# Bilinear block with channels on the partitions, and a mode sum with the products standing

## The chip, the cores and the metric

One core of one Trainium2 chip. The metric is the device time of one execution, in microseconds. TensorE is called PE below (PEld its weight loads), VectorE DVE, ScalarE ACT, GpSimd POOL, and SyncE, which only issues DMAs here, SP. All data is fp32; an fp32 matmul appears in the trace as two MATMUL records.

## The reference, cut to what matters

The input is 16 images of 56 x 56 pixels with 128 channels. Four residual blocks follow each other: windowed attention, a triangle product, a Fourier attention operator, and a bilinear block. Each is fed by a group norm. The two blocks that the change touches:

```python
# block 3 (Fourier): out is the attention-weighted sum over 32 heads, projd a spectral convolution of it
attn_w = softmax(q k^T)                                   # per head, 56 x 56
out    = einsum('bhts,bhsd->bhtd', attn_w, v)
projd  = irfft2(sum over heads of rfft2(out) * wP) + skip # the "mode sum", then the inverse transform
# ... two more spectral operators, each ending in an inverse transform

# block 4 (bilinear)
xp = silu(x @ W1) @ W2                                    # 128 + 16 + 16 channels: q (8 heads x 16), k, v
q, k, v = l2norm(q per head), l2norm(k), l2norm(v)
K_H1    = conv3x7(k, H1_w) + P1                           # per pixel 16 x 16
kernel  = einsum('xnk,xkd->xnd', q, K_H1)
feature = conv3x7(v, H2_w); V_G = conv3x7(v, G_w) + I     # per pixel 16 x 16 each
feature = einsum('xvw,xvd->xwd', V_G, feature)
out     = einsum('xnd,xvd->xvn', kernel, feature)         # 128 channels
```

## The kernel before, in words

`tile_blocks` loads constants and weights once, then runs the images one after the other: load and transpose, the four blocks, store. An image lies in SBUF as 128 channels by 3136 pixels; most loops run over 7 chunks of 448 pixels. SBUF and PSUM tiles come from rotating pools: `big` (6 tiles), `w8`, `w5`, `w4`, `w2`, `sm`, and in PSUM `psb` (4 single banks) and `psd` (2 pairs of banks). A framework places the waits and a scheduler fixes, at build time, the order of each engine's instructions; every engine then takes its queue in order. The order on PE is nearly that of the program, with a few later matmuls slipped in where an earlier one would wait.

`_fourier`. After the attention (L938 scores) the weights of 32 heads lie in `at` as 16 pairs. L979 makes the modes of the values (copied by ACT at L980, doubled to 112 partitions by one SBUF-to-SBUF DMA), L1005 and L1010 add the skip path. The mode sum: for each quarter q of 448 modes and each pair of heads, two DMAs spread the coefficient `table` over 56 partitions each, DVE or POOL (every third pair) makes three products of 448 (L1030, L1032: a complex product written with three real ones), and six matmuls (L1037) with the attention weights as the stationary operand (112 rows, 64 columns) sum them. Two pairs go to the two 64-column halves of PE. L1048 combines the three sums and L1051 folds the halves. `inverse` turns modes into pixels: L828 (32 stationary columns; neighbours in the order lie in different 32-column groups) and L839 (32 rows; neighbours in different row groups). It runs three times, the first time with one part in place of two.

`_bilinear`. First loop, the projections: per chunk L1107 (x W1, Silu on ACT), L1113 and L1114 (times W2, pixels on the partitions), squares and sums for the norms (L1117, L1118), the power -1/2 on POOL (L357, by way of `power`), scaling (L1127, L1128), transposes of k and v (L1131), a copy to `pad` (L1134), and 14 DMAs that build `im`, the 7-fold shifted image. Second loop, the products: per group of 112 pixels L1149 makes the three convolutions with pixels on the partitions, and `contract` runs three times, each a product of 2048 (L1160) and a reduction over 16 (L1161); the third product is POOL's. L1171 and L1172 add the residual.

Of the kernel before, what the change touches and what calls it, by code (L numbers as in the profile page):

```python
# [33 lines left out]
P = 128  # L36
# [49 lines left out]
def _constants():  # L86
# [71 lines left out]
    c["eyedup"] = ed  # L158
    c["fold"] = np.concatenate([np.eye(T), np.eye(T)], 0)
    c["unpair"] = ed.T  # L160
# [12 lines left out]
def _weights(i):  # L173
# [71 lines left out]
    wk3 = np.zeros((113, 3, 16, 16), np.float32)  # L245
    wv3 = np.zeros((113, 3, 2, 16, 16), np.float32)
    for u in range(16):
        for kw in range(7):
            wk3[u * 7 + kw, :, :, u] = h1[u, :, :, kw].T
            wv3[u * 7 + kw, :, 0, u, :] = h2[:, :, kw].T  # L250
            wv3[u * 7 + kw, :, 1, :, u] = gg[:, :, kw].T
    wk3[112, 1] = g["L3_conv_P1"][0].T
    wv3[112, 1, 1] = g["L3_conv_I"][0].T
    w["l3wk"] = wk3.reshape(113, -1)
    w["l3wv"] = wv3.reshape(113, -1)
# [17 lines left out]
def tile_blocks(ctx: ExitStack, tc: tile.TileContext, ins, out, at, stages=(0, 1, 2, 3)):  # L273
# [9 lines left out]
    w5p = ctx.enter_context(tc.tile_pool(name="w5", bufs=2))  # L283
    w8p = ctx.enter_context(tc.tile_pool(name="w8", bufs=3))
    w4p = ctx.enter_context(tc.tile_pool(name="w4", bufs=3))
    w2p = ctx.enter_context(tc.tile_pool(name="w2", bufs=6))
    smp = ctx.enter_context(tc.tile_pool(name="small", bufs=6))
# [14 lines left out]

    def w5():
        return w5p.tile([P, 3 * CH], F32, tag="w5", name=uid("w5_"))
# [50 lines left out]
    def power(dst, src, p, n):  # L355

        ptt(dst, src, C("mhalf")[:p, :n], ALU.pow)  # L357

# [300 lines left out]
def _fourier(env):  # L659
# [63 lines left out]
    table = e.dpool.tile([32, 4, 3, CH], F32, tag="table", name="table")  # L723
# [19 lines left out]

    stt(tmp, cvr, -1.0, cvi, ALU.mult, ALU.subtract)
    tt(cvi, cvi, cvr, ALU.subtract)
    for c, v in enumerate((cvr, cvi, tmp)):
        nc.sync.dma_start(out=table[:, :, c, :], in_=v.rearrange("p (c n) -> p c n", n=CH))
# [68 lines left out]
    def inverse(parts, consume):  # L816


        halves = [v.rearrange("p (l t) -> p t l", t=T) for v in parts]
        last = len(halves) - 1  # L820
        for k in range(2):
            ng = 4 - k
            p = e.psd()
            for i in range(8):
                for c, half in enumerate(halves):
                    for g in range(ng):
                        o = p[32 * g : 32 * g + 32, i // 4, i % 4 * TT : (i % 4 + 1) * TT]
                        mm(o, lhsT=half[:, 32 * k + 8 * g + i, :], rhs=C(f"di{c + 1}"), start=c == 0, stop=c == last)  # L828
# [4 lines left out]
            for g0 in range(0, ng, 2):  # L833
                gs = range(g0, min(g0 + 2, ng))
# [368 lines left out]
```

## Time and profile before

| | us |
|---|---|
| median of 3 runs | 23861.55 (23851.68 to 23864.71) |
| the profiled execution's own time | 23861.55 |
| its span, first to last instruction | 23859.8 |
| PE / DVE / POOL / ACT busy | 13641.5 / 12171.6 / 6721.9 / 3478.3 |
| mean granted clock of PE | 0.692 |

The profile page gives the busy time of each engine over the span, groups of instructions by line, and the idle time before each group with what ended it. Windows give the same busy times inside a stretch, with the clock that was granted to PE (1.00 is full speed, 0.50 half) and the DMA share. Busy time of PE counts overlapped matmuls once; the mean length of one is longer than the distance between two.

### The profile page before, as it was taken

The page shows a single profiled execution, that of the slowest core. Times are in us where ns is not written, and L with a number is a line of the kernel's source. Part 1 is how long each engine was busy: PE and PEld are TensorE (multiplying, and loading weights), DVE is VectorE, ACT ScalarE, POOL GpSimd, SP SyncE. Part 2 cuts the span into 40 slices and gives each one's busy share as a digit, 9 for nine tenths or more (in the row PEclk, how much of TensorE's full clock was granted, in tenths as well). Part 3 has the DMA queues.
Part 4 walks back from the last instruction along what each step waited for, and adds up shares of the span by engine and source line. Part 5 has one row for each costly group of instructions (what it writes and reads, how often), then busy time and mean ns, then how long its engine had stood idle before and what let it go on. Part 6 is the DMA issues. An engine that isn't in the chain of part 4 may idle for free. (4 is left out here: it accounts for less than half of the span.)

```text
span 23859.8 us, 190705 instructions
## 1 busy us (share of the span) xinstructions
PE 13641.5 (57%) x77186; PEld 7738.1 (32%) x77186; DVE 12171.6 (51%) x12638; ACT 3478.3 (15%) x6016; POOL 6721.9 (28%) x3295
## 2 busy tenths in 40 slices
PE   6556465564645647456475564745647456474564
PEld 4233242332423324233142332423324233242331
DVE  4364644646446464464644646446464464644646
ACT  2111121110211102111021110211102111021110
POOL 1322313133131331313313133131331313313133
PEclk7767676676766767667676676766767667676676
DMA  0202002020020200202011020110200102011020
GB/s 25 61 7 66 7 17 58 7 66 7 24 51 7 66 8 25 50 7 66 8 27 48 7 66 10 27 46 7 66 10 25 47 7 66 10 27 46 7 66 8
DMA packets 478015, 744.96 MB, mean 31 GB/s; under 512 B 259922, under 2 KB 361170, under 8 KB 475986
## 3 DMA queue, kind: packets, MB, share of 16 engines
q1 hardware_dynamic: 476994, 730.54, 12.3%
q8 instruction: 611, 10.01, 0.2%
q14 instruction: 266, 2.18, 0.0%
q10 hardware_dynamic: 144, 2.22, 0.0%
HBM read 648.35 MB, written 26.38 MB: 28 GB/s over the span
## 5 line engine op out<-in xcount | busy, mean ns | idle before, releaser
L1149 PE MATMUL psb<-wgt,big 113*112 113x256 f32 (+1 forms) x5376 | 2871.9, 704 | 2738.6 <-DVE w L1160 2281.6
L1161 DVE TENSOR_REDUCE w<-w 112x128 f32<-112x2048 f32 x1344 | 3031.6, 2282 | 1147.0 <-POOL w L1160 1101.5
L357 POOL TENSOR_TENSOR sm<-sm,cst 112x40 f32<-112x40 f32 (+2 forms) x272 | 1680.4, 6178 | 6467.2 <-DVE sm L374 2979.9
L1160 POOL TENSOR_TENSOR w<-w,w 112x2048 f32<-112x2048 f32 x448 | 2020.6, 4510 | 4324.3 <-DVE w L1161 4074.2
L1149 PEld LDWEIGHTS psb<-wgt,big 113*112 113x112 f32 x5376 | 1357.2, 265 | 4176.5 <-DVE w L1160 2605.2
L1037 PE MATMUL psd<-w,w 112*64 112x448 f32 x4096 | 1603.7, 661 | 343.8 <-POOL w L1032 322.1
L1030 DVE TENSOR_TENSOR w<-big,w 112x448 f32<-112x448 f32 x688 | 540.7, 788 | 1569.5 <-PE psd L1037 918.3
L1037 PE MATMUL psb<-w,w 112*64 112x448 f32 x2048 | 1083.2, 673 | 271.1 <-POOL w L1030 235.2
L1030 POOL TENSOR_TENSOR w<-big,w 112x448 f32<-112x448 f32 x336 | 399.2, 1188 | 2562.7 <-PE psd L1037 993.6
L1151 ACT COPY w<-psb 112x512 f32<-112x512 f32 x448 | 262.2, 585 | 5591.7 <-PE psb L1149 2950.1
L1160 DVE TENSOR_TENSOR w<-big,psb 112x2048 f32<-112x2048 f32 x448 | 1020.2, 2277 | 52.0 <-PE psb L1149 52.0
L1160 DVE TENSOR_TENSOR w<-w,w 112x2048 f32<-112x2048 f32 x448 | 1025.8, 2290 | 37.6 <-DVE w L1161 0.9
L536 PE MATMUL psb<-cst,w 128*49 128x128 f32 x2048 | 460.8, 418 | 849.8 <-DVE w L530 849.8
L1037 PEld LDWEIGHTS psd<-w,w 112*64 112x64 f32 x4096 | 418.1, 157 | 1432.3 <-POOL w L1032 593.3
L934 POOL TENSOR_TENSOR w<-w,coef 128x448 f32<-128x448 f32 x512 | 654.5, 1294 | 560.4 <-DVE head L935 296.7
L1032 DVE TENSOR_TENSOR w<-big,w 112x896 f32<-112x896 f32 x688 | 796.4, 1158 | 0.0
L938 PE MATMUL psd<-w,head 128*64 128x56 f32 x8192 | 642.9, 238 | 231.0 <-DVE head L935 231.0
L799 PE MATMUL psb<-cst,big 128*56 128x64 f32 (+1 forms) x5376 | 416.8, 254 | 620.0 <-ACT big L787 376.5
L654 POOL TENSOR_TENSOR big<-big,w 128x448 f32<-128x448 f32 x112 | 126.0, 1131 | 2166.7 <-DVE w L653 2166.7
L1032 POOL TENSOR_TENSOR w<-big,w 112x896 f32<-112x896 f32 x336 | 734.7, 2187 | 0.0
L1131 PE MATMUL psb<-cst,w 112*32 112x112 f32 x448 | 115.8, 382 | 1048.4 <-DVE w L1128 1048.4
L536 PEld LDWEIGHTS psb<-cst,w 128*49 128x49 f32 x2048 | 397.4, 201 | 905.9 <-issue 891.4
(241 smaller groups left out, 23018.2 us busy)
## 6 DMA issues: line engine op xcount, KB each, us to landing
w<-table SPq DMA_DIRECT2D x2048, 294.0 KB
big<-pad SPq DMA_DIRECT2D x1568, 28.0 KB
w<-x SPq DMA_DIRECT2D x112, 224.0 KB
out<-w SPq DMA_DIRECT2D x112, 224.0 KB
big<-big SPq DMA_DIRECT2D x16, 784.0 KB
cst<-cst SPq DMA_DIRECT2D x1, 2246.5 KB
wgt<-wgt ACTq DMA_DIRECT2D x1, 2170.5 KB
big<-late SPq DMA_DIRECT2D x4, 224.0 KB
```

The costliest lines, as they stand in the source:

```text
L357: ptt(dst, src, C("mhalf")[:p, :n], ALU.pow)
L536: nc.tensor.transpose(p[:WIN, i * P : (i + 1) * P], s3[:, 4 * g + i, :], C("ident"))
L799: mm(p[:T, i * 2 * nl : (i + 1) * 2 * nl], lhsT=src[:, t * T : (t + 1) * T], rhs=fc, start=True, stop=True)
L934: ptt(t3, xb, bc(coef[:, 1, h, :], 2, T), ALU.mult)
L938: mm(sp[half : half + 64, bank, col : col + T], lhsT=hd[:, l, :], rhs=yk[:, l, :], start=l == 0, stop=False)
L1030: eng.tensor_tensor(t[:TT, :CH], x3[0][:, s], tb[:TT, :CH], ALU.mult)
L1032: eng.tensor_tensor(t2, ri3[:, :, s], b2, ALU.mult)
L1037: mm(acc[k][64 * half : 64 * half + 64, :], lhsT=at[:, pair % 8, pair // 8, :], rhs=t[:TT, k * CH : (k + 1) * CH], start=two == 0, stop=tw ...
L1149: mm(p[:TT, :m], lhsT=t[:113, c0 : c0 + TT], rhs=W(w)[:, dr * m : (dr + 1) * m], start=dr == 0, stop=dr == 2)
L1151: nc.scalar.copy(fv[:TT, :], pv[:TT, :])
L1160: eng.tensor_tensor(t4, x, y, ALU.mult)
L1161: reduce(dst, t4, AX.X, ALU.add)
```

## The change

The words of the change speak of the bilinear block; the diff rewrites the mode sum and `inverse` too.

- Bilinear products: channels stay on the partitions. Each convolution (`conv`) gives 256 channels by 448 pixels as two matmul groups, copied by ACT. In `contract`, PE replicates each head-pair's 16 values over the partitions with a constant 0/1 matrix (`rep`, 32 rows), DVE multiplies straight from PSUM, and PE sums over 16 partitions with another (`red`, 32 columns). The three contractions are taken in a pipeline over the chunks. POOL has no product here any more.
- Projections: q comes with channels on the partitions; its norms are taken by a matmul with `heads` and applied at the very end. The power on POOL becomes `rsqrt`, ten small DVE operations.
- Mode sum: two real products in place of three, `table` with two parts; the product of 896 is the stationary operand (8 slices of 112 columns) and the attention weights move (56 columns). DVE makes the first part's product, POOL the second's. Two pairs of heads share a table DMA.
- `inverse`: the loop over the column groups is outside, so neighbours in the order lie in the same group; in the second step the two parts of one group follow each other.
- Pools: `w5` is gone, `w4` has 5 tiles, `sm` 8.

```diff
-    w5p = ctx.enter_context(tc.tile_pool(name="w5", bufs=2))
-    w4p = ctx.enter_context(tc.tile_pool(name="w4", bufs=3))
+    w4p = ctx.enter_context(tc.tile_pool(name="w4", bufs=5))
-    smp = ctx.enter_context(tc.tile_pool(name="small", bufs=6))
+    smp = ctx.enter_context(tc.tile_pool(name="small", bufs=8))
...
+    def rsqrt(dst, src, p, n):
...
+        ts(y.bitcast(I32), src.bitcast(I32), -0.5, float(0x5F3759DF), ALU.mult, ALU.add)
+        for i in range(3):
+            tt(t, y, y, ALU.mult)
+            stt(t, t, -0.5, src, ALU.mult, ALU.mult)
+            stt(dst if i == 2 else y, t, 1.5, y, ALU.add, ALU.mult)
...
     inverse:
-            for i in range(8):
-                for c, half in enumerate(halves):
-                    for g in range(ng):
-                        o = p[32 * g : 32 * g + 32, i // 4, i % 4 * TT : (i % 4 + 1) * TT]
-                        mm(o, lhsT=half[:, 32 * k + 8 * g + i, :], rhs=C(f"di{c + 1}"), start=c == 0, stop=c == last)
+            for g in range(ng):
+                for i in range(8):
+                    t = 32 * k + 8 * g + i
+                    o = p[32 * g : 32 * g + 32, i // 4, i % 4 * TT : (i % 4 + 1) * TT]
+                    for c in range(2):
+                        mm(o, lhsT=halves[c][:, t, :], rhs=C(f"di{c + 1}"), start=c == 0, stop=c == 1)
...
-            for g0 in range(0, ng, 2):
-                gs = range(g0, min(g0 + 2, ng))
-                ps = [e.psb() for _ in gs]
-                for c, name in enumerate(("fir", "fii")):
-                    for g, p in zip(gs, ps):
-                        s = slice(32 * g, 32 * g + 32)
-                        mm(p[:, :CH], lhsT=C(name)[s, :], rhs=v4[s, c], start=c == 0, stop=c == 1)
...
+            for g in range(ng):
+                s = slice(32 * g, 32 * g + 32)
+                p = e.psb()
+                mm(p[:, :CH], lhsT=C("fir")[s, :], rhs=v4[s, 0], start=True, stop=False)
+                mm(p[:, :CH], lhsT=C("fii")[s, :], rhs=v4[s, 1], start=False, stop=True)
...
     mode sum:
-                    eng = nc.gpsimd if n % 3 == 2 else nc.vector
...
-                    eng.tensor_tensor(t[:TT, :CH], x3[0][:, s], tb[:TT, :CH], ALU.mult)
...
-                    eng.tensor_tensor(t2, ri3[:, :, s], b2, ALU.mult)
...
-                            lhsT=at[:, pair % 8, pair // 8, :],
-                            rhs=t[:TT, k * CH : (k + 1) * CH],
...
+                for c, eng in ((0, nc.vector), (1, nc.gpsimd)):
+                    o = pair % 2 * 896 + c * CH
+                    t = e.w4()
+                    eng.tensor_tensor(
+                        t[:TT, :896].rearrange("p (l c r) -> p l c r", l=8, c=2),
+                        x4,
+                        bc(tb[:TT, o : o + CH].rearrange("p (l r) -> p l r", l=8), 2, 2),
+                        ALU.mult,
+                    )
+                    for l in range(8):
                         mm(
+                            acc[c][:TT, l * T : (l + 1) * T],
+                            lhsT=t[:TT, l * TT : (l + 1) * TT],
+                            rhs=at[:, pair % 8, pair // 8, :T],
...
     bilinear:
+    def conv(w, im, q):
+        t = e.w4()
+        for h in range(2):
+            p = e.psb()
+            for dr in range(3):
+                c0 = (8 * q + dr) * T
+                mm(p[:, :CH], lhsT=W(w)[:, (2 * dr + h) * P : (2 * dr + h + 1) * P], rhs=im[:113, c0 : c0 + CH], start=dr == 0, stop=dr == 2)
+            nc.scalar.copy(t[:, h * CH : (h + 1) * CH], p[:, :CH])
+        return t[:, : 2 * CH].rearrange("p (h t) -> p h t", h=2)
+
+    def contract(y, z):
+        acc = e.psb()
+        for n in range(2):
+            prods = []
+            for two in range(2):
+                p = e.psd()
+                for i in range(2):
+                    s = slice(64 * two + 32 * i, 64 * two + 32 * i + 32)
+                    mm(p[:, i, :CH], lhsT=C("rep")[s, n * P : (n + 1) * P], rhs=y[s], start=True, stop=True)
+                t = e.w8()
+                t4 = t[:, : 4 * CH].rearrange("p (i h t) -> p i h t", i=2, h=2)
+                tt(t4, bc(p[:, :, :CH], 2, 2), bc(z, 1, 2), ALU.mult)
+                prods += [t4[:, 0], t4[:, 1]]
+            for h in range(2):
+                for i, t in enumerate(prods):
+                    mm(
+                        acc[32 * i : 32 * i + 32, :CH],
+                        lhsT=C("red")[:, (2 * n + h) * 32 : (2 * n + h + 1) * 32],
+                        rhs=t[:, h],
...
-            for a in range(4):
-                n = 4 * q + a
-                pk, pv = e.psb(), e.psb()
-                for p, t, w, m in ((pk, im[0], "l3wk", 256), (pv, im[1], "l3wv", 512)):
...
-                contract(nc.vector, kern, bc(q4[:, n], 2, D), bc(k3, 1, NH))
-                contract(nc.vector, s3, bc(kern, 2, D), bc(f3, 1, NH))
-                contract(nc.gpsimd, o3, bc(s3, 1, D), bc(g3, 2, NH))
...
+        for q in range(NCH + 2):
+            if q < NCH:
+                kern[q] = evacuated(contract(qc[:, q * CH : (q + 1) * CH], conv("l3wk", im[0], q)))
+            if 0 <= q - 1 < NCH:
+                feat[q - 1] = evacuated(contract(kern.pop(q - 1), conv("l3wf", im[1], q - 1)))
+            if 0 <= q - 2:
+                last(q - 2, feat.pop(q - 2))
```

In the projections, two wide matmuls a chunk (W2 with 128 columns) give q with channels on the partitions, and twelve short ones give k, v (32 columns) and the sums of squares of q (8 columns). `evacuated` is an ACT copy out of PSUM; `last` adds four transposes and a DVE product with the norms of q.

## The prediction

> **What bounds the kernel now.** I read the page's busy line first, then the busy time in stretches of one image, then the costliest groups, the waits inside the two stages that change, and the timeline.
>
> ```profile
> span 23859.8 us, 190705 instructions
> PE 13641.5 (57%) x77186; PEld 7738.1 (32%) x77186; DVE 12171.6 (51%) x12638; ACT 3478.3 (15%) x6016; POOL 6721.9 (28%) x3295
> ```
>
> No engine is full: each stage has its own bound. Stretches of the second image (us; busy PE, PEld, DVE, ACT, POOL; granted clock; DMA share; GB/s), in order: work ahead of the mode sum, mode sum, first inverse transform, bilinear projections, bilinear products:
>
> ```profile
> 1987.50:2065.90 78.40, 70.56 (x309) 57.09 (x309) 13.65 (x20) 12.88 (x23) 4.40 (x4) 0.50 0.10 26
> 2065.90:2261.00 195.10, 149.41 (x441) 44.29 (x440) 81.34 (x91) 4.26 (x8) 68.94 (x42) 0.87 0.71 183
> 2261.00:2276.20 15.20, 10.32 (x140) 6.86 (x140) 5.46 (x9) 1.06 (x2) 0.00 (x0) 0.72 0.00 1
> 2504.80:2633.20 128.40, 61.64 (x166) 25.05 (x166) 17.14 (x49) 14.98 (x26) 47.19 (x7) 0.59 0.11 16
> 2633.20:3037.00 403.80, 190.33 (x399) 94.16 (x398) 324.47 (x164) 20.96 (x37) 127.80 (x33) 0.67 0.04 10
> ```
>
> The last stretch is VectorE's: 324 of 404 us busy, the rest mostly waits for POOL's product (63 us in that stage's waits). Its groups (the last one by shape, inside 2504.8 to 2633.2):
>
> ```profile
> L1161 DVE TENSOR_REDUCE w<-w 112x128 f32<-112x2048 f32 x1344 | 3031.6, 2282 | 1147.0 <-POOL w L1160 1101.5
> L1160 DVE TENSOR_TENSOR w<-big,psb 112x2048 f32<-112x2048 f32 x448 | 1020.2, 2277 | 52.0 <-PE psb L1149 52.0
> L357 POOL TENSOR_TENSOR sm<-sm,cst 112x40 f32<-112x40 f32 x7 | 47.2, 6741 | 80.2 <-DVE sm L1119 80.2
> ```
>
> The projections are one serial chain per chunk, 18.0 us from one L1107 to the next in the timeline, 6.74 of it POOL's power. The mode sum is spread over DMA (0.71), PE, VectorE and POOL.
>
> [...] The trace agrees on the two states, but shows which work counts as busy (start, length, then the columns above):
>
> ```profile
> 1990.00:2010.00 20.00, 20.00 (x109) 20.00 (x108) 1.14 (x1) 3.67 (x7) 0.00 (x0) 0.50 0.00 1
> 1935.00:1975.00 40.00, 29.62 (x402) 26.16 (x401) 40.00 (x46) 0.00 (x0) 27.94 (x23) 1.00 0.01 1
> ```
>
> The first is L979 (56 rows, 112 columns moved): PE is never idle, yet stays at half. The second, L938 (128 rows), has gaps and full clock. Columns moved[...], times rows used: [...] 0.22 of full-speed capacity; [...] 0.47. I tallied the granted-clock record in its 3.41 us steps, leaving out lines whose tiles run side by side: of 1378 half-clock steps below 0.30 none was followed by full clock; at 0.35 to 0.375, 8 in 10 were. Of full-clock steps at 0.40 or more, nine in ten stayed. [...] L1051, 112 stationary and 56 moving columns, gives the price of such a stream:
>
> ```profile
> 2210.82 1.75 PE L1051 MATMUL psb<-cst,w 128*112 128x56 f32 x16 [1.41 <-DVE w L1048]
> 8050.06 3.02 PE L1051 MATMUL psb<-cst,w 128*112 128x56 f32 x15 [1.41 <-DVE w L1048]
> ```
>
> An fp32 matmul is two records here. Start to start, 98 ns at full clock ((1.75 - 0.262)/15), 187 ns at half ((3.02 - 0.393)/14)[...]. [...] matmuls on different 32-column groups run together[...]. L828 agrees: 560 records an image in 23.1 us busy, 41 ns each at 317 ns long. [...]
>
> **The change, per image (16 of them, one after the other).**
> *Mode sum.* Out: 192 matmuls of 448 columns, POOL's third of the products, a third of the table's bytes. In: 4 x 16 pairs x 2 parts x 8 = 1024 matmuls, 2048 records of 112 stationary, 56 moving columns. VectorE's product of 896 costs 1.16 us a pair (L1032), POOL's 2.19: 140 us a stage; table DMA, two thirds of 195 x 0.71 = 139, is 92 us. PE is last whatever its clock: 2048 x 187 = 383 us at half, 2048 x 98 = 201 at full. Which? At half the stream counts [...] 0.22: never raised in the tally. At full it counts 0.42: kept. So the entry decides, and the stretch ahead is at 0.50; its matmuls (L979, L1005, L1010) stay, and the order lists put nothing else among the new ones. I take half: 384 with the evacuation, against 195.1, less some 3 us by which the stretch ahead gets shorter (a few of the sum's matmuls were issued inside it): +186. If at full: 202, so +4. Bounds: these two, as a stream that is kept or never raised has no third state. Products and DMA issues (SP's table loads fall from 128 to 64 an image) are hidden by this PE stream; POOL's 140 us would show only if PE took less. The three-way sum at the stage's end (L1048, L1051, L1052, 3 us a quarter) and POOL's 4 additions L987 go; they are inside the 195.
> *Inverse transforms (three).* Now all 16 matmuls of one column group precede the next group's, so they no longer overlap; the first also gets 112 in place of 56. 224 records x 98 = 22.0, plus some 45 records at half clock at the two starts (+4), plus the second step, whose row groups now follow each other: 5 + 4 slots of 0.75 = 6.8, copies between 1.7: 34.5 us each. Before, L828 to L839 measured 12.8, 13.9 and 13.5 (means of 16). +63. Bounds: +30 if groups still overlap in part, +85 at half clock throughout.
> *Projections.* PE's order takes the chunks strictly one after the other, transposes last, so the chain's length is the pitch and each wait holds the next chunk's L1107 behind it. POOL's 6.74 goes; in its place ten small VectorE operations in a row, 0.2 each (L1119 0.18) = 2.0. L1113/L1114 (3.9) become four wide records at clock mixed (2.2) and 24 short ones (2.5 to 4), with two ScalarE passes (0.8 exposed). With L1107 (3.4), the reduction and its neighbours (1.1), one broadcast product (0.3) and the transposes (1.3) the chain is 3.4 + 2.2 + 0.8 + 3.0 + 1.1 + 2.0 + 0.3 + 1.3 = 14.1 to 14.5 in place of 18.0: 7 x 3.7 = -26. The 98 im2col DMAs and their order on SP stay. Bounds -40 and -5.
> *Products.* Out: VectorE's 84 reductions and 56 products, POOL's 28. In: 21 contractions, each 4 VectorE products (8.1 us), 6 convolution, 8 replicating and 16 summing matmuls of 448 columns, 0.75 each at full clock alone: 6 x 0.75 = 4.5; 8 in pairs on different rows 3.0; 16, which the order splits into 2 and 6 at a time, 4.5: 12.0. Both engines hand work back and forth through two PSUM pairs. PE takes its queue in order, so a sum that waits for a product holds the replications and convolutions queued behind it, and VectorE waits for those. Following the listed order at full clock: products 1 and 2 end at 3.0 and 5.0, 3 at 7.1, 4 at 9.6 (its replication waits behind six sums), the last sums at 11.1, then five convolution matmuls, on which the next product waits: 14.8. Its count is (4.5 x 113/128 + 3.0 x 0.5 + 4.5)/14.8 = 0.67, so full clock mostly; some steps fall (the first 3.4 us count 0.32): 15.5. 21 x 15.5 = 326, transposes and final products 14, next image's load and start 12: 352, against 404 (first L1149 to the next image's L481): -52. Bounds: 12.3 a contraction if the queues overlap (-119); 24 at half clock (+126).
> The rest (constants, one-time table, deeper pools; the other stages' order is the same but for VectorE swaps): nothing; these run in chains, so a freed buffer is no one's last wait; at most 5 either way.
> Sum: 186 + 63 - 26 - 52 = +171; x 16 = 2736. On the profiled execution's 23861.55 us (span 23859.8 and 1.75 around it; it is the median run too): 26,600.
>
> **The rivals.** *A: full clock in the mode sum* (ends faster). For: at full the stream would hold itself. Against: the 0.50 at entry. With the first inverse also starting at full (-5): +4 + 58 - 26 - 52 = -16 an image: 23,600. It decides from a mean record spacing of 104 ns: then the stage is 213 us and the image even. *B: contractions overlap*, 12.3 us: 67 less an image, 25,500. For: two PSUM pairs; against: the order's blocks. *C: contractions at half clock*, PE 24 us each: 29,450. For: L1149 now sits at 0.67; against: dense 448-column work.
>
> **How the numbers follow.** Main 0.62 (own range 25,700 to 27,700), A 0.13, B 0.17, C 0.08. PREDICTED is main's time. The range 24,600 to 27,900 takes B and the bounds of inverses and projections and leaves out A, C and main's tails. No change means within 0.2%, 48 us, about what measurement can tell: only A's edge, 0.02. Faster 0.11, slower 0.87.
>
> **What would show it.** Clock 0.50 and one unbroken PE stream of about 384 us in the mode sum; inverses of some 34 us; projection chunks near 14; contractions of 15 to 16 with VectorE half idle. A mode sum near 200 us, or contractions away from 12 to 18, makes it wrong.

## The result, and the profile after

The changed kernel takes 27,052.9 us (median of 4 runs, 27,007.5 to 27,080.6) against 23,856.6 us (4 runs, 23,833.5 to 23,864.7): 1.134 times the time, 95% interval 1.132 to 1.1359. The prediction was 26,600 us, range 24,600 to 27,900. Direction, range and the main mechanism hold; two terms of the sum are off by more than 20 us an image, in opposite directions.

The page of the changed kernel: TensorE is busy for 20,702 us in place of 13,642, VectorE and POOL for less than before.

```profile
span 27005.7 us, 278225 instructions
PE 20702.2 (77%) x121154; PEld 14441.2 (53%) x121154; DVE 9763.5 (36%) x12268; ACT 3813.4 (14%) x6800; POOL 4892.4 (18%) x3023
```

The stretches of the second image that answer to those of before (us; busy PE, PEld, DVE, ACT, POOL; granted clock; DMA share; GB/s), in the same order: work ahead of the mode sum, mode sum, first inverse, projections, products:

```profile
2182.60:2258.20 75.60, 65.63 (x299) 56.17 (x298) 12.61 (x18) 12.88 (x23) 4.11 (x2) 0.50 0.09 22
2258.20:2640.80 382.60, 382.60 (x2050) 382.45 (x2050) 68.25 (x63) 3.73 (x7) 128.67 (x62) 0.50 0.24 60
2640.80:2675.00 34.20, 25.56 (x254) 22.72 (x254) 10.62 (x11) 1.59 (x3) 0.00 (x0) 0.85 0.00 0
2923.30:3030.60 107.30, 80.90 (x260) 44.20 (x261) 22.29 (x104) 18.95 (x40) 0.00 (x0) 0.61 0.12 19
3030.60:3434.00 403.40, 346.88 (x1343) 111.58 (x1342) 187.66 (x116) 37.92 (x72) 2.47 (x7) 0.84 0.04 10
```

Read the second line first: PE is busy for all of its 382.6 us, and the clock that was granted meanwhile is 0.50. The last line is the one that surprised: the same length as before, but now PE is busy for 347 of 403 us and VectorE for 188, and the clock is 0.84, not full. The costliest groups:

```profile
L1041 PE MATMUL psb<-w,w 112*112 112x56 f32 x32768 | 6120.6, 393 | 0.0
...
L1114 DVE TENSOR_TENSOR w<-psd,w 128x1792 f32<-128x1792 f32 x1344 | 2689.2, 2022 | 2770.6 <-PE psd L1111 2272.9
...
L1118 PE MATMUL psb<-w,cst 128*32 128x448 f32 x10752 | 2259.6, 687 | 751.8 <-DVE w L1114 746.7
```

The mode sum (L1041) alone is 6,121 us, with no idle time ahead of it. VectorE's products (L1114) have as much idle time ahead of them as work, and it is the replications L1111 that end most of it; the sums L1118 in turn wait for those products. Two engines wait for each other.

By stages, from the first and last matmul of each stage in the two traces, mean over the images, in us:

| stage of one image | before | after | change | predicted |
|---|---|---|---|---|
| window attention and triangle | 373.6 | 373.7 | +0.1 | 0 |
| scores to the end of the skip path | 144.9 | 145.0 | +0.1 | -3 |
| mode sum | 194.7 | 382.4 | +187.7 | +189 |
| three inverses | 40.2 | 80.0 | +39.8 | +63 |
| projections | 128.1 | 106.6 | -21.5 | -26 |
| products, store, next load | 404.1 | 395.3 | -8.8 | -52 |
| whole image | 1488.1 | 1685.7 | +197.6 | +171 |

(The +186 of the prediction is the second and third row together; the stages that are not listed change by 0.2 together.) 197.6 x 16 = 3,162, against 3,146 between the two profiled spans.

### The profile page after: what moved, and what is told of

Its sections match the earlier page's. It is cut to its first block, busy times and chain, and to the rows that moved or that the text cites. A ratio compares the mean times of both kernels' runs of the same rounds, so it can differ in the third digit from the quotient of the medians.

```text
span 27005.7 us, 278225 instructions
## 1 busy us (share of the span) xinstructions
PE 20702.2 (77%) x121154; PEld 14441.2 (53%) x121154; DVE 9763.5 (36%) x12268; ACT 3813.4 (14%) x6800; POOL 4892.4 (18%) x3023
## 5 line engine op out<-in xcount | busy, mean ns | idle before, releaser
L1041 PE MATMUL psb<-w,w 112*112 112x56 f32 x32768 | 6120.6, 393 | 0.0
L1041 PEld LDWEIGHTS psb<-w,w 112*112 112x112 f32 x32768 | 6117.8, 307 | 1.7
L1114 DVE TENSOR_TENSOR w<-psd,w 128x1792 f32<-128x1792 f32 x1344 | 2689.2, 2022 | 2770.6 <-PE psd L1111 2272.9
L1034 POOL TENSOR_TENSOR w<-big,w 112x896 f32<-112x896 f32 x1024 | 2136.7, 2087 | 5224.7 <-PE psb L1041 3602.6
L1118 PE MATMUL psb<-w,cst 128*32 128x448 f32 x10752 | 2259.6, 687 | 751.8 <-DVE w L1114 746.7
L363 POOL TENSOR_TENSOR sm<-sm,cst 128x56 f32<-128x56 f32 (+1 forms) x160 | 925.1, 5782 | 7328.6 <-DVE sm L393 4645.9
L1098 PE MATMUL psb<-big,wgt 113*128 113x448 f32 x4032 | 1725.0, 570 | 0.0
L1118 PEld LDWEIGHTS psb<-w,cst 128*32 128x32 f32 x10752 | 416.3, 123 | 2308.8 <-DVE w L1114 1253.7
L1098 PEld LDWEIGHTS psb<-big,wgt 113*128 113x128 f32 x4032 | 753.6, 198 | 930.9 <-issue 916.9
L843 PEld LDWEIGHTS psd<-cst,big 112*32 112x32 f32 x10752 | 1002.1, 139 | 101.8 <-DVE big L865 56.3
L843 PE MATMUL psd<-cst,big 112*32 112x112 f32 x10752 | 1035.7, 270 | 22.9 <-DVE big L865 22.9
L1111 PE MATMUL psd<-w,cst 32*128 32x448 f32 x3584 | 847.1, 641 | 0.0
L950 PEld LDWEIGHTS psd<-w,head 128*64 128x64 f32 x8192 | 655.5, 168 | 227.0 <-DVE head L947 197.6
```

The source lines that it names most:

```text
L843: mm(o, lhsT=halves[c][:, t, :], rhs=C(f"di{c + 1}"), start=c == 0, stop=c == 1)
L950: mm(sp[half : half + 64, bank, col : col + T], lhsT=hd[:, l, :], rhs=yk[:, l, :], start=l == 0, stop=False)
L1034: eng.tensor_tensor(t[:TT, :896].rearrange("p (l c r) -> p l c r", l=8, c=2), x4, bc(tb[:TT, o : o + CH].rearrange("p (l r) -> p l r", l=8 ...
L1041: mm(acc[c][:TT, l * T : (l + 1) * T], lhsT=t[:TT, l * TT : (l + 1) * TT], rhs=at[:, pair % 8, pair // 8, :T], start=pair == 0 and l == 0, ...
L1098: mm(p[:, :CH], lhsT=W(w)[:, (2 * dr + h) * P : (2 * dr + h + 1) * P], rhs=im[:113, c0 : c0 + CH], start=dr == 0, stop=dr == 2)
L1111: mm(p[:, i, :CH], lhsT=C("rep")[s, n * P : (n + 1) * P], rhs=y[s], start=True, stop=True)
```

## The experiments

Theory: (1) the mode sum is slow only because it is entered at half clock and its stream (112 rows, 56 columns moved for each 112 loaded) can't raise it; (2) the inverses lost overlap by the order of their matmuls; (3) the contractions lose by TensorE's waits for products, and more than the waits themselves, since the clock falls in them. Rivals stand in each expectation. All runs start from the changed kernel unless they say otherwise; the kernel before took 23,846.5 to 23,867.2 us beside them. The stage means of the runs, in us an image, read from their traces as above:

| run | mode sum | inverses | projections | products | image |
|---|---|---|---|---|---|
| changed kernel | 382.4 | 80.0 | 106.6 | 395.3 | 1685.7 |
| burst, 128 rows | 209.4 | 78.3 | 106.8 | 398.2 | 1515.1 |
| burst, 56 rows | 392.4 | 80.1 | 106.9 | 396.8 | 1697.1 |
| bilinear block alone | 195.7 | 38.8 | 106.7 | 395.5 | 1461.7 |
| inverse as before | 382.4 | 39.2 | 106.7 | 396.1 | 1643.3 |
| convolution early | 382.4 | 79.7 | 107.2 | 332.8 | 1624.0 |
| deeper order | 382.4 | 80.0 | 106.8 | 287.9 | 1578.2 |
| filler of four | 382.4 | 80.3 | 105.9 | 408.7 | 1700.0 |
| filler of two | 382.4 | 79.8 | 107.1 | 387.1 | 1677.9 |
| all three edits | 209.3 | 36.7 | 105.7 | 287.7 | 1358.2 |
| before's Fourier, deeper order | 195.9 | 38.9 | 105.9 | 289.0 | 1351.6 |

(A burst is counted in the mode sum. The kernel before has 194.7, 40.2, 128.1, 404.1 and 1488.1.)

### The entry clock of the mode sum

```diff
         p12 = e.big()
+        p = e.psb()
+        for i in range(6):
+            mm(p[:, :CH], lhsT=C("cen"), rhs=xa[:, i * CH : (i + 1) * CH], start=True, stop=True)
         for q in range(4):
```

> Added to the changed kernel: six 128-row, 448-column matmuls right ahead of the mode sum of each image, into a PSUM tile that nothing reads. Theory (the mode sum stays at half clock only because it is entered at half, and its 56-row stream can hold full clock but not regain it): granted clock in the mode sum 0.9 to 1.0, spacing of its records 98 to 105 ns in place of 187, the stage 205 to 215 us in place of 382, the burst itself 5 to 10 us, so about -165 us an image: 24,400 us, between 24,200 and 24,700. Rival 1 (this stream cannot hold full clock whatever it is entered at): the clock falls back to half within some 10 us, the stage stays at 375 to 385 us, and the burst comes on top: 27,050 to 27,250. Rival 2 (the spacing is set by something other than the clock, the products or the table's transfers): clock full, but spacing above 130 ns: 25,500 or more.

(The stream that this expectation calls 56-row has 112 rows and moves 56 columns.) Measured: 24,191.6 us (24,149.6 to 24,276.2, 4 runs; 1.0141 of before, 1.012 to 1.0162), 8 us under the theory's band. The windows of its second image, ahead of the burst, the burst, the mode sum (columns as above):

```profile
2010.00:2085.50 75.50, 65.45 (x298) 55.89 (x297) 12.64 (x19) 12.74 (x23) 4.10 (x2) 0.50 0.09 22
2086.05:2093.50 7.45, 7.42 (x13) 3.61 (x14) 0.00 (x0) 0.00 (x0) 0.00 (x0) 0.62 0.00 0
2093.50:2295.00 201.50, 201.50 (x2050) 201.44 (x2049) 85.56 (x62) 3.72 (x7) 129.07 (x62) 1.00 0.45 113
```

The control uses 56 rows of the same matmuls (`C("cen")[:T]`, `xa[:T, ...]`).

> The control of the burst: the same six matmuls of 448 columns at the same place, but over 56 rows in place of 128; nothing reads their result. Theory (the clock is granted by moved columns weighted by their rows, and 56 of 128 rows at half clock are a share of 0.22): the clock stays at 0.5, the mode sum at 382 us, the burst adds some 9 us an image: 27,150 to 27,250 us. Rival (any stretch in which TensorE is busy without a gap gives full clock): as with 128 rows, 24,200 to 24,700. Second rival (it was only a shift in time that helped): both bursts the same.

Measured: 27,177.8 us (2 runs; 1.1388 of before, 1.1365 to 1.1411), 125 us over the changed kernel. Its second image, the same three stretches:

```profile
2200.00:2275.50 75.50, 65.54 (x298) 56.04 (x298) 12.60 (x18) 12.89 (x23) 4.12 (x2) 0.50 0.09 22
2276.20:2285.50 9.30, 9.29 (x13) 3.88 (x13) 0.00 (x0) 0.00 (x0) 0.00 (x0) 0.50 0.00 0
2285.50:2668.00 382.50, 382.50 (x2050) 382.40 (x2050) 67.70 (x62) 3.72 (x7) 128.92 (x62) 0.50 0.23 60
```

In both runs PE is busy without a gap in burst and mode sum, and the 2048 records of the mode sum are the same. The only difference is how many rows the six matmuls used. With 128 the clock is 1.00 for all of the next 201.5 us (98 ns a record), with 56 it is 0.50 for all of 382.5 (187 ns). Theory 1 holds: the entry decides, the stream keeps the clock that it finds, and being without gaps did not raise the clock (0.50 over all of the 382.5 us); the rows of the burst did.

Two further runs give the dose. In one the burst has another length in each image, in the other six matmuls use another number of rows in each image:

```diff
+        p = e.psb()
+        for i in range((0, 1, 2, 3, 4, 5, 6, 8)[b % 8]):
+            mm(p[:, :CH], lhsT=C("cen"), rhs=xa[:, i % 7 * CH : (i % 7 + 1) * CH], start=True, stop=True)
```

```diff
+        p, n = e.psb(), (56, 64, 72, 80, 88, 96, 104, 112)[b % 8]
+        for i in range(6):
+            mm(p[:, :CH], lhsT=C("cen")[:n], rhs=xa[:n, i * CH : (i + 1) * CH], start=True, stop=True)
```

> The changed kernel with a burst ahead of the mode sum (128 rows, 448 columns, read by nobody) of another length in each image: 0, 1, 2, 3, 4, 5, 6 and 8 matmuls in images 1 to 8, and again in images 9 to 16. At half clock one takes 1.5 us, and the granted clock is recorded in steps of 3.41 us. Theory (one step in which the moved columns, weighted by rows, are over about 0.35 of the full rate turns the clock up; a burst step gives up to 0.5, the mode sum's own 0.22): no image with 0 or 1 turns (382 us), those with 3 or more all turn (200 to 212 us), with 2 it depends on how the burst falls on the steps; 10 to 12 of 16 images turn, total 27,053 - 175 x 10 to 12: 24,950 to 25,350 us. Rival (the burst must last over two steps or more, some 7 us): only 5, 6 and 8 turn, 6 of 16 images, 26,000 us.

> The changed kernel with a burst of six 448-column matmuls ahead of the mode sum (read by nobody) over another number of rows in each image: 56, 64, 72, 80, 88, 96, 104 and 112 in images 1 to 8, and again in images 9 to 16. Theory (the share is 0.5 x rows / 128 at half clock, and about 0.35 is needed): 56 to 80 rows (0.22 to 0.31) do not turn the clock, 96 to 112 (0.375 to 0.44) do, 88 (0.34) either way; 6 to 8 images of 16 turn, total 27,178 - 183 x 6 to 8: 25,700 to 26,080 us. Rival 1 (it takes all 128 rows): none turns, 27,180. Rival 2 (anything over the stream's own 56 rows is enough, for it is the change that counts): 14 turn, 24,620.

Measured, one run each: 25,239.7 and 26,062.7 us, both in the theory's bands. The mode sums, read from the trace image by image, fall on two values with nothing between:

| burst | images | mode sum, us |
|---|---|---|
| 0, 1 or 2 matmuls of 128 rows | 6 | 382.4 to 382.5 |
| 3 matmuls | 2 | 202.0, 202.1 |
| 4, 5, 6 or 8 matmuls | 8 | 201.5 |
| six of 56, 64, 72, 80 or 88 rows | 10 | 382.4 to 382.5 |
| six of 96, 104 or 112 rows | 6 | 201.5 |

As the windows of the run with lengths show it (image 3, two matmuls; image 4, three):

```profile
3958.90:4341.30 382.40, 382.40 (x2050) 382.26 (x2048) 67.74 (x62) 3.72 (x7) 128.54 (x62) 0.50 0.24 60
5643.10:5845.20 202.10, 202.10 (x2050) 202.03 (x2049) 85.66 (x62) 3.72 (x7) 129.03 (x62) 1.00 0.44 113
```

and of the run with rows (image 5, 88 rows; image 6, 96):

```profile
7364.80:7747.20 382.40, 382.40 (x2050) 382.30 (x2049) 67.72 (x62) 3.72 (x7) 128.71 (x62) 0.50 0.24 60
9063.00:9264.50 201.50, 201.50 (x2050) 201.44 (x2049) 87.70 (x62) 3.72 (x7) 131.67 (x62) 1.00 0.45 113
```

At half clock 88 rows are a share of 0.5 x 88/128 = 0.344 and 96 rows 0.375, so the turn lies between these two, at or a little above the 0.35 of the tally of before. The clock is recorded in steps of 3.41 us, and full clock began on a step's boundary, 3.6 or 5.6 to 5.9 us after the burst's first matmul. Three matmuls take 4.6 us and turned the clock in both images that had three. Two take 3.1 us, nearly as long as a step, but in both images a boundary cut them in two: the steps that hold the parts have shares of 0.32 and 0.30 in the one image, 0.33 and 0.29 in the other. Two that lie within one step would give it (0.5 x 2.98 + 0.22 x 0.43)/3.41 = 0.46, an estimate from these figures (one takes 1.49 us at half clock); no run has that case.

The traces allow a sharper tally than the prediction's. Take each step of 3.41 us and give it this share: the time in which columns move, times the rows in use out of 128, times the granted clock, over the step. A column of a record takes 0.84 ns at full clock and 1.67 ns at half: in the changed kernel, records of 448 columns on 113 rows (L1098) start 376 and 747 ns apart (medians). (Matmuls that run side by side count their rows once if they share them, as on different column groups, and added up if they do not; starts are moved by 0.1 us.) In these traces the next step is then at full clock when the share is 0.375 or more and at half when it is less, whatever the clock was before, with 271 exceptions in 102,980 steps. All 14 traces together:

| clock of a step | its share | steps | next step at full clock |
|---|---|---|---|
| half | under 0.375 | 49,085 | 156 |
| half | 0.375 or more | 10,136 | 10,108 |
| full | under 0.375 | 10,237 | 23 |
| full | 0.375 or more | 33,522 | 33,458 |

The 0.375 and the shift were fitted on the traces of the two kernels (41 exceptions in 14,867 steps); the other 12 follow them (230 in 88,113). All but 23 of the exceptions lie within 0.015 of 0.375. So in these traces one line serves for rising and falling, and the one step ahead is enough to tell. The mode sum lies below the line at half clock (0.5 x 56 x 1.67/187 x 112/128 = 0.22) and above it at full (56 x 0.84/98 x 112/128 = 0.42), and it kept either: 0.50 for 382.5 us, 1.00 for 201.5. The prediction's shares for L979 and L938 follow from the same times: 0.5 x 56/128 = 0.22, as 112 columns at 1.67 ns fill the 187 ns from one record to the next, and 402 x 56 x 0.84 ns in 40 us = 0.47.

### One half of the change alone

> The bilinear block of the change with the Fourier block of before, so one half of the change alone; two image pads in the bilinear block in place of three, and the pools of before (three 4 KB tiles in place of five), because the two blocks do not fit side by side otherwise. Theory (the two halves of the change are independent, as the stage table of the two traces says: projections -21.4 us, products -8.8 us an image): 23,857 - 16 x 30 = 23,370 us, between 23,200 and 23,500. Rival 1 (my prediction's own sizes, -26 and -52 us, hold when the Fourier block of before leaves clock and buffers as they were): 22,600. Rival 2 (the third pad and the fourth and fifth 4 KB tile carried the gain): within 0.3% of before, 23,800 to 23,900.

The edit puts `_fourier`, its table and its `w5` pool back, and fits the pools (`w4` 3, `sm` 6, `pads` 2). Measured: 23,421.0 us (4 runs; 0.9813 of before, 0.9796 to 0.9829), 51 over the theory's figure (the window attention and triangle, 377.6 us an image in place of 373.6, are more than that). Projections 106.7 and products 395.5 us are those of the full change, so the halves are independent: the bilinear block gains some 440 us, the Fourier block loses some 3,600. Rival 1, the prediction's own sizes, is out by 800 us. The gain is there without the deeper pools (rival 2).

### The order in the inverses

```diff
-            for g in range(ng):
-                for i in range(8):
...
-                    for c in range(2):
+            for i in range(8):
+                for c, half in enumerate(halves):
+                    for g in range(ng):
```

> The changed kernel with the inverse of before for all three uses: the two matmuls of one output one after the other, four outputs of one row group in a row, rather than the changed order. Theory (the 40 us an image that the three inverses gained come from the new order of their matmuls, or from its two parts, and not from the clock at which they are entered): each inverse back from 26.8/27.4/25.8 to 34.5 us as I had predicted or near it in the opposite case. In numbers: if the order is what made them slower, inverses 13 to 18 us, -30 to -40 us an image, 26,410 to 26,570 us. If the inverse of the changed kernel is slower only because it has two parts where before had three (before's order is its own), no gain: within 0.3% of the changed kernel, 26,970 to 27,130. If the clock at entry decides (half after the mode sum, full in the other two), the first stays at 26 us and the other two fall to 13: 26,620.

The first sentence of this expectation describes the two orders the wrong way round: it is the changed kernel that has the two matmuls of one output one after the other, and this run puts the column groups innermost again, as the diff shows, and the second step's pairs of row groups as well. The numbers are those meant. Measured: 26,338.6 us (26,330.5 to 26,379.3, 4 runs), 714 us or 44.6 an image under the changed kernel, 71 below the theory's band. All three inverses fall to 12.6 to 13.6 us, so the clock at entry (the third forecast) is not what made them slow. The first inverse of the second image in the timeline (start, length, count), changed kernel:

```profile
2640.71 14.15 PE L843 MATMUL psd<-cst,big 112*32 112x112 f32 x144
...
2655.12 1.06 PE L851 MATMUL psb<-w,cst 32*128 32x448 f32 x8 [0.25 <-ACT w L846]
2655.97 0.95 PE L852 MATMUL psb<-w,cst 32*128 32x448 f32 x8
2656.86 7.28 PE L843 MATMUL psd<-cst,big 112*32 112x112 f32 x80
...
2665.48 1.04 PE L851 MATMUL psb<-w,cst 32*128 32x448 f32 x6 [1.34 <-ACT w L846]
```

and with the order of before:

```profile
2602.04 6.04 PE L844 MATMUL psd<-cst,big 112*32 112x112 f32 x166
...
2608.26 1.80 PE L855 MATMUL psb<-w,cst 32*128 32x448 f32 x16 [0.18 <-ACT w L847]
2609.99 2.15 PE L844 MATMUL psd<-cst,big 112*32 112x112 f32 x58
...
2613.66 1.92 PE L855 MATMUL psb<-w,cst 32*128 32x448 f32 x12 [1.51 <-ACT w L847]
```

The same 224 records of the first step take 14.15 + 7.28 = 21.4 us in the one order and 6.04 + 2.15 = 8.2 us in the other, 13.2 us apart. Three times that is 39.6 of the 40.8 us an image by which the three inverses get shorter: theory 2 is shown. Matmuls on different column groups overlapped here: they start 37 ns apart on average (8.2 us / 224), while the 112 columns of one take 94 ns at full clock (112 x 0.84); neighbours of one group start 96 ns apart (21.4 / 224). The second step takes 1.8 to 1.9 us each time in both: in the changed kernel, too, the scheduler has put four L851 (8 records) in a row and then four L852, so neighbours are in different row groups, whatever the source says. The prediction had followed the source.

### The contractions

One contraction of the changed kernel in the timeline:

```profile
3200.84 1.01 PE L1111 MATMUL psd<-big,cst 32*128 32x448 f32 x2
...
3201.51 3.96 DVE L1114 TENSOR_TENSOR w<-psd,w 128x1792 f32<-128x1792 f32 x2 [3.63 <-ACT w L1099]
3203.68 1.71 PE L1118 MATMUL psb<-w,cst 128*32 128x448 f32 x4 [1.83 <-DVE w L1114]
3205.32 1.86 PE L1111 MATMUL psd<-big,cst 32*128 32x448 f32 x4
3207.11 3.20 PE L1118 MATMUL psb<-w,cst 128*32 128x448 f32 x12
3207.23 2.02 DVE L1114 TENSOR_TENSOR w<-psd,w 128x1792 f32<-128x1792 f32 x1 [1.76 <-PE psd L1111]
3210.24 1.02 PE L1111 MATMUL psd<-big,cst 32*128 32x448 f32 x4
...
3211.31 2.02 DVE L1114 TENSOR_TENSOR w<-psd,w 128x1792 f32<-128x1792 f32 x1 [2.06 <-PE psd L1111]
...
3213.77 1.70 PE L1118 MATMUL psb<-w,cst 128*32 128x448 f32 x12
3215.40 3.27 PE L1098 MATMUL psb<-big,wgt 113*128 113x448 f32 x8
```

PE waits 1.83 us for the first product (the expectations below say some 4). The step of the clock that holds this wait, 3200.0 to 3203.4, has 0.84 us of convolution on 113 rows and 0.75 us of replication on 32: (0.84 x 113/128 + 0.75 x 32/128)/3.41 = 0.27, below the line. From 3203.4 to 3210.2 the granted clock is 0.5: two replications take 1.86 us rather than 1.02, the six sums (x12) 3.20 rather than the 1.70 that the second group of six takes. The next contraction begins at 3218.61: 17.8 us. Two edits change only the order in which PE gets this work. The first puts the next contraction's convolution behind the first four replications; the second also takes the third pair of replications ahead of the first eight sums, and one half of the convolution to the end. `ready` holds the convolution issued in the contraction before, `start` sets up the next one as a generator of two halves:

```diff
     def contract(y):
+        z = ready.pop()
+        start()
...
-            sums(acc, n, prods)
+            if n == 0:
+                for _ in going[0]:
+                    pass
+            sums(acc, n, prods)
```

```diff
+        p0 = product(y, z, 0, 0) + product(y, z, 0, 1)
+        next(going[0], None)
+        p1 = product(y, z, 1, 0)
+        sums(acc, 0, p0)
+        p1 += product(y, z, 1, 1)
+        next(going[0], None)
+        sums(acc, 1, p1)
```

> The changed kernel, one edit in the bilinear block: the convolution of the next contraction is issued right behind the first four replications of this one, where TensorE waits for the first two products, rather than ahead of its own replications. The work is the same. Theory (a contraction takes 17.7 us rather than my 15.5 because TensorE waits some 4 us for the first products, its clock falls to half in that wait, and the sums and replications behind it run at 0.95 to 1.1 us in place of 0.54 to 0.64): the wait is filled, the clock stays full, the contraction falls to 14 to 15.5 us, -45 to -80 us an image: 25,800 to 26,350 us. Rival 1 (hand-over between VectorE and the two PSUM pairs paces the contraction; where the convolution stands is no matter): within 10 us an image, 26,900 to 27,100. Rival 2 (ScalarE's eviction of the convolution, which VectorE's product needs, was late): gain, but with the clock as it was.

> The changed kernel with a deeper order in the bilinear block: half of the next convolution behind the first four replications, the third pair of replications ahead of the first eight sums, the other half of the convolution behind the last pair of replications. The work is the same. Theory (both of a contraction's waits for products are what it loses, by themselves and by the clock): contraction near the 12.3 us of TensorE's own work plus transposes, 13 to 14.5 us, -70 to -105 us an image: 25,370 to 25,950 us, and 30 us an image less than with the convolution early alone. Rival 1 (VectorE's 4 x 2.02 us and the hand-over pace it): as the other, or no gain at all, 26,900 to 27,100. Rival 2 (three product tiles are too few for this order: the fourth product waits for the first sums): not better than the convolution early alone.

Measured: 26,005.3 us (25,993.2 to 26,034.5, 4 runs), and 25,305.6 us (25,286.8 to 25,317.4, 4 runs), 65 and 109 us an image less than the changed kernel; the first is in its band, the second 64 us below it. A stretch of the second image's products, first with the convolution early, then in the deeper order:

```profile
2978.00:3273.00 295.00, 267.60 (x1206) 93.04 (x1204) 164.66 (x88) 32.77 (x62) 0.10 (x1) 0.93 0.03 7
2927.00:3180.00 253.00, 252.11 (x1238) 88.05 (x1240) 166.64 (x90) 33.11 (x63) 0.10 (x1) 0.99 0.04 8
```

The clock rises from the 0.85 of the changed kernel to 0.93 and 0.99, so the gain is not that of a late copy by ScalarE with the clock as it was (rival 2 of the first). A contraction in the deeper order:

```profile
3056.24 1.04 PE L1120 MATMUL psd<-w,cst 32*128 32x448 f32 x8
...
3057.21 2.52 PE L1099 MATMUL psb<-big,wgt 113*128 113x448 f32 x6
3057.37 5.89 DVE L1123 TENSOR_TENSOR w<-psd,w 128x1792 f32<-128x1792 f32 x3 [3.08 <-PE psd L1120]
3059.66 1.02 PE L1120 MATMUL psd<-w,cst 32*128 32x448 f32 x4
...
3060.61 2.46 PE L1129 MATMUL psb<-w,cst 128*32 128x448 f32 x16
3063.00 1.02 PE L1120 MATMUL psd<-w,cst 32*128 32x448 f32 x4
3063.95 2.52 PE L1099 MATMUL psb<-big,wgt 113*128 113x448 f32 x6
...
3066.41 1.71 PE L1129 MATMUL psb<-w,cst 128*32 128x448 f32 x16
3068.05 1.03 PE L1120 MATMUL psd<-w,cst 32*128 32x448 f32 x8
```

No PE line in it has an idle time in brackets, three products run back to back (5.89 us), and the next contraction begins 11.8 us later. Here PE's own work is the bound (busy for 252 of 253 us): the 12.3 us that the prediction gave for rival B was a good price for a case that the written order doesn't reach. So the order, not VectorE's hand-over, paced the changed kernel.

How much of this was the wait, and how much the clock? Two runs fill the wait with matmuls that nothing reads, four as in this diff or two, and leave the order:

```diff
                 prods += [t4[:, 0], t4[:, 1]]
+            if n == 0:
+                p = e.psb()
+                for i in range(4):
+                    mm(p[:, :CH], lhsT=C("cen"), rhs=z.rearrange("p h t -> p (h t)")[:, :CH], start=True, stop=True)
```

> The changed kernel with four 128-row, 448-column matmuls added in every contraction right behind the first four replications, where TensorE waits for products; nothing reads their result, and the convolution stays where it was. It tells the clock's part of the contraction's loss from the wait's: the wait stays as long, only filled. Theory (the filler, about 3 us at full clock, keeps the clock full over the wait of some 4 us, and the sums and replications behind it run at 0.54 to 0.64 us rather than 0.95 to 1.1): -20 to -45 us an image, 26,330 to 26,730 us, granted clock in the products 0.95 or more in place of 0.84. Rival 1 (the clock is a symptom; what counts is the wait): no gain, and with the filler longer than the wait up to +20 us an image, 27,050 to 27,370. Rival 2 (all of what the early convolution gained, 62 us an image, was the clock): 26,060.

> As the run with the filled wait, but two filler matmuls (128 rows, 448 columns, read by nobody) in each contraction in place of four: about 1.5 us at full clock, where TensorE's idle time in the changed kernel is 44 us an image, 2.1 us a contraction. With four, idle time fell by 16 us an image, the changed sums and replications by 45, and the fillers themselves took 65. Theory (the clock is a loss of its own, and the filler of four was only longer than the gap): fillers 33 us, idle time down by 10 to 20, sums and replications shorter by 25 to 45: -10 to -30 us an image, 26,570 to 26,890 us. Rival (two are too few to keep the clock up over the wait; granted clock stays near 0.85): fillers 33 less idle time 10 to 20, +10 to +25 us an image, 27,200 to 27,450.

Measured: 27,233.4 us with four (27,232.1 to 27,242.7, 4 runs), 26,904.5 us with two (26,891.1 to 26,915.4, 4 runs); 181 above and 148 below the changed kernel. With four the theory's time missed, and the time is the one that rival 1 gave; but its reason does not hold. The window of the products and the group of the sums inside it (after the bar: busy us, mean ns, then idle ahead), second image, changed kernel:

```profile
3030.60:3402.10 371.50, 327.80 (x1261) 102.49 (x1259) 170.73 (x92) 33.23 (x63) 0.10 (x1) 0.85 0.03 7
```

```profile
L1118 PE MATMUL psb<-w,cst 128*32 128x448 f32 x640 | 137.8, 701 | 43.7 <-DVE w L1114 43.4
```

filler of four (L1119 is the filler):

```profile
3045.00:3421.60 376.60, 348.52 (x1421) 121.00 (x1420) 168.97 (x92) 33.33 (x64) 0.10 (x1) 0.95 0.03 7
```

```profile
L1122 PE MATMUL psb<-w,cst 128*32 128x448 f32 x640 | 115.0, 592 | 28.1 <-DVE w L1114 27.8
...
L1119 PE MATMUL psb<-w,cst 128*128 128x448 f32 x160 | 65.4, 551 | 0.0
```

filler of two:

```profile
3019.60:3381.10 361.50, 330.61 (x1341) 110.39 (x1339) 169.44 (x92) 33.33 (x63) 0.11 (x1) 0.95 0.03 7
```

```profile
L1122 PE MATMUL psb<-w,cst 128*32 128x448 f32 x640 | 113.7, 585 | 30.9 <-DVE w L1114 29.6
...
L1119 PE MATMUL psb<-w,cst 128*128 128x448 f32 x80 | 35.3, 564 | 0.0
```

Both fillers raise the clock from 0.85 to 0.95, and the steps at half clock in a products stage fall from 32 to 16 with four and 12 with two (means of 15 images). Work that was not touched gets shorter: the sums from 137.8 to 115.0 and 113.7 us, the replications (L1111, two groups, 49.9 + 36.2 before) to 63.6 and 78.1. With two: -24.1 (sums) - 8.0 (replications) - 12.8 (idle) + 35.3 (filler) = -9.6 us, and the image got 7.8 shorter by the stage means, 9.3 by the medians (148.4/16). With four the filler is 65.4 and the rest -60.9 in this image, whose stage is a long one in the changed kernel (402.6 us, mean 395.3); over 15 images the filler takes 68.7, sums and replications lose 40.9 and PE's idle time 16.4, and the stage is 13.4 longer: a filler longer than the gap. With two, TensorE did more work and the kernel was faster: the clock's part, 32 us an image in sums and replications, is more than what the filler costs beyond the idle time that it covers (35.3 - 12.8); the means of 15 images, 31.5 and 37.1 - 14.5, say the same. Theory 3 is shown. The run with two is 15 us outside the theory's band, 300 from the rival's. The early convolution does the same with useful work.

### All together

> The changed kernel with three things together: the burst of six 128-row matmuls ahead of the mode sum (read by nobody), the inverse in the order of before, and the deeper order of the contractions. Theory (the three are independent): -178.8 x 16 for the burst, -44.6 x 16 for the inverses, -70 to -105 x 16 for the contractions off 27,053: 21,800 to 22,360 us, under both kernels. Rival (a stage that is entered at full clock only because of the one before loses it in the new order): up to 26 us an image are given back, 22,800 at most.

> The Fourier block of before (as in the run with the bilinear block alone: two pads, three 4 KB tiles) with the changed bilinear block in the deeper order of contractions. Theory: 23,421 less 70 to 105 us x 16: 21,740 to 22,300 us, within 0.5% of the run with all three edits on the changed kernel. Rival (three 4 KB tiles in place of five hold back the convolution that is issued early): gain of half that, 22,600 to 22,900.

Measured: 21,787.5 us (21,777.1 to 21,794.8, 4 runs; 0.913 of before, 0.9117 to 0.9144) and 21,674.1 us (21,664.9 to 21,715.8, 4 runs; 0.9086 of before, 0.9073 to 0.91). Both are faster than both kernels; the edits add up to what they gave one by one, within 57 us for the first (27,052.9 - 2,861.3 - 714.3 - 1,747.3 = 21,730) and 1 us for the second (23,421.0 - 1,747.3), each a little better than its band. Three 4 KB tiles in place of five held back nothing (the second's rival, 22,600 us or more). The new mode sum with its burst (209.3 us) stays behind that of before (195.9); what is worth keeping of the change is the bilinear block, in the deeper order.

## Why the prediction was right, and where it was not

*Mode sum, right by its own steps.* +187.7 for +189. The price of 187 ns a record, the share of 0.22 at half clock and the entry at 0.50 gave the stage to within 2 us; rival A was the same stream entered at full clock, and the runs with a burst are that rival made real, at 201.5 us for its 202. The range was rightly not a mean of the two. (The bracket for 98 ns gives 99 as it is written, as the first spacing is longer; 98 is the usual one. In the tally, with columns counted while they move, 12 of 139 half-clock steps at 0.35 to 0.375 rose and not 8 in 10, and all 1,640 full-clock steps at 0.40 or more stayed, not nine in ten; 0.22 and 0.42 are far enough from the line for this not to matter.)

*Inverses, mechanism right, size off: +39.8 for +63.* The term was 34.5 us each, measured 26.8, 27.4 and 25.8. Of the 7.8 us, 3.2 are the second step, priced at 6.8 and measured at 3.6: the prediction followed the source, where one column group's two parts follow each other, and not the order that the scheduler made of it. Another 4.4 are the first step, priced at 22.0 + 4 and measured at 21.6: only 18 of its 224 records start at half clock on average, not 45 (850 in 48 inverses), and at full clock they are some 88 ns apart on average, not 98. The bound of +30 "if groups still overlap in part" covered it.

*Projections, right: -21.5 for -26.* The pitch is 15.3 us a chunk on average, for 14.1 to 14.5. The 24 short records take 5.4 us in a chunk on average (3.9 where all of them are at full clock), where 2.5 to 4 was the term; the rest of the chain was shorter than its terms.

*Products, the step that failed: -8.8 for -52.* The prediction followed the order of the queue rightly (two sums, a replication, six sums) but timed it "at full clock", with 0.7 us for steps that fall. VectorE's product was priced rightly: the 8.1 us for four were the author's estimate, and four at the measured 2,022 ns (L1114) are 8.09. In the contraction shown, product 3 ends 8.4 us after the start (its 7.1), product 4 at 12.5 (its 9.6), the last sums at 14.6 (its 11.1), the whole 17.8 (its 15.5). The first two of these slips are PE work at half clock behind a wait; the last sums lose another 0.6 us at full clock, and the convolution behind them takes 3.1 where the order at full clock had 3.7. The share of 0.67 over a whole contraction is no guide where, as tallied above, the share of each step of 3.41 us goes with the clock of the next: 32 of the 116 steps of such a stage are at half clock, on average of 15 images, each behind a step of 0.37 or less. The prediction had itself noted that the first 3.4 us count only 0.32. A part of rival C (half clock) so entered the main case. 43 us an image too little here and 23 too much in the inverses, with smaller terms, left 453 us of 27,053: that the total is within 2% is partly luck.

## What to carry to other kernels

A dense stretch of matmuls is not at full clock for being dense: here two that used 56 of 128 rows, or loaded 112 columns of weights for every 56 columns moved, were entered at half clock and stayed there without a gap (0.50 for 20.0 us of L979 and for the 382.6 us of the mode sum). Look at the granted clock where such a stretch begins, and put work on more rows ahead of it (here three matmuls of 128 rows, 4.6 us, were worth 180). Between dense matmuls a wait of some 2 us was paid twice here, once as idle time (1.83 us) and once by the clock of the step behind it (two replications 1.86 us in place of 1.02, six sums 3.20 in place of 1.70), so fill it with matmuls that don't depend on the other engine. And read neighbours in the order that the scheduler made, not in the source: whether they lie in the same column group or in different ones was worth a factor of 2.6 in the inverse's first step, and in the second step the scheduler had undone what the source said.

## What the runs showed of the hardware beyond that

VectorE's product of 896 takes 1.09 us in the mode sum at half clock (67.70 us for 62) and 1.38 on average with the burst (85.56 for 62), while POOL's stays at 2.08. This is not TensorE's clock as such: in the run with the burst of six, 414 of the 1,024 products share less than 0.3 us with an operation of POOL and take 1.09 us, and 602 share 0.6 to 0.9 us and take 1.58, within the same stage; in the changed kernel none shares any time with POOL. The shorter stage brings the two engines' products together. No run varies that alone, and in the kernel before 20 products that shared 0.3 to 1.2 us with POOL still took 1.08 (43 that shared 1.8 or more took 2.29), so which operations of POOL cost VectorE time stays open. What a burst shorter than six would give beside the other edits was not tried.
